# A graph block's head: the first linear layer in parts of 128, 256, 384 and 482 nodes, with its order of work written anew

## The chip, the cores and the metric

The kernel runs on one core of a Trainium2 chip, as a single launch. A core has a matrix engine (TensorE, PE in the profile; PEld is its loading of weights), a vector engine (VectorE, DVE), an activation engine (ScalarE, ACT), GpSimd (POOL) and SyncE (SP), which issues most of the DMAs here. Each runs its own queue of instructions and waits for the others by semaphores. The metric is the device time of the launch in microseconds (us).

## The reference

1250 nodes with 512 features go through a layer norm, a graph network of two layers with a linear layer ahead, a linear attention beside it, and a gated feed-forward layer. What the change touches is the beginning of this, the head:

```
xn  = _layernorm(x, axis=-1)                    # 1250 x 512
h   = xn @ lin_W.T + lin_b
h   = where(h > 0, h, lin_a * h)                # PReLU, the linear layer
for l in range(2):
    agg = segment_sum(h[src], dst, 1250)        # 41250 edges, sorted by dst
    h   = (h + agg) -> linear, PReLU, linear -> batch norm -> relu
k   = softmax over the nodes of (xn @ w_k) ...  # attention, uses xn too
```

The kernel turns the edge list into a dense matrix of 1250 x 1250 counts (adj, identity included), so that the sum over edges becomes a matrix product. For this it needs, of each block of 512 edges, its smallest and largest target node.

## The kernel before

**Tiles.** The nodes are cut in ten tiles of 128 (the last has 98). For a tile t, `x_first(t)` takes mean and variance (bn_stats and bn_aggr on VectorE, a Sqrt on ScalarE), `x_second(t)` makes scale and bias from them (a reciprocal and one more small step on VectorE) and normalizes the 128x512 tile on ScalarE into `xn`, and `x_third(t)` turns it: four transposes on TensorE into one PSUM bank and one ScalarE copy of 128x512 into `xn_t`, where features lie on the partitions (`to_features`, L602 to L607).

**Linear layer.** `lin(c0, cn, f)` (L710) computes output features f*128 to f*128+127 for the nodes from c0 to c0+cn: four products, which the chip runs as eight matmuls, into one bank, then `prelu` (L609): two ScalarE Relus from that bank (of the value and of its negative) and a VectorE step that joins them. It needs the copies in `xn_t` of all tiles from c0 to c0+cn. The nodes are taken in four parts, 256, 256, 384 and 354 wide, each for f from 0 to 3: sixteen calls.

**Edge chain.** Between them stand the steps that lead from the loaded edge list to the keys by which blocks are built: e_d, a cast of the targets on ScalarE (L746); smallest and largest target per partition on VectorE (L748 to L751); a transposition of both on TensorE (L759) and a reduction into `span` (L762); a transposition that spreads them over the partitions (L771, L772); from these base, base_i, low, key, s_hi and s_lo on VectorE and ScalarE (L766 to L794).

**Blocks.** `weave(us)` (L820) makes as many of the 81 edge blocks as are due: 0.70 blocks for each microsecond it is told. A block is two sets of one-hot rows, oh_s (4 of 128x128) and oh_k (4 of 128x240), made on VectorE; for every third block from the fifth on, oh_s comes from ScalarE instead (`source_rows`). Two made blocks are kept back (`keep=2`); then TensorE multiplies the oldest (four matmuls, L849) and VectorE adds it into adj (L851).

**Order.** From L718 (`given(engines={PE, DVE, Activation})`) to `head.close()` the order on TensorE, VectorE and ScalarE is the order in which the program is written: each of the three runs its own instructions of the head in that order, one behind the other. After `head.close()` the order is set by the framework. SP issues the loads at L653 to L675: tiles 0 and 1 of x, a quarter of the linear weights, tile 2, a quarter, tile 3, two quarters, the edges, tiles 4 to 9, and then weights of later stages. GpSimd clears adj (L685) and writes its diagonal. `stay_warm(n)` is n transposes of a constant on TensorE, read by nobody.

```
    for f in range(1, DT):
        weave(1.4)
        lin(512, 384, f)
        if f < 3:
            x_third(f + 7)
    head.close()
    for f in range(DT):
        weave(2.4)
        lin(896, 354, f)
```

Behind the head come the attention's products with wk, in whose midst most of the blocks are woven in (L878 and after).

Of the kernel before, what the change touches and what calls it, by code (L numbers as in the profile page):

```python
# [9 lines left out]
F32 = mybir.dt.float32  # L10
# [7 lines left out]
P = 128  # L18
N = 1250
D = 512  # L20
DT = D // P
# [20 lines left out]
CHUNKS = [(0, 418), (418, 416), (834, 416)]  # L42


def rows(t):
    return min(P, N - t * P)
# [479 lines left out]
def usual_block(  # L526
# [23 lines left out]
    nc = tc.nc  # L550
# [3 lines left out]
    tmp = ctx.enter_context(tc.tile_pool(name="tmp", bufs=2))  # L554
# [7 lines left out]
    def bank(dtype=F32):  # L562
        return psum.tile([P, 512], dtype, tag="bank", name="bank")

    def large(place, shape, dtype=F32, name="large"):

        return big.tile(shape, dtype, tag=place, name=name)

    def weight(src, name):
        w = wpool.tile([P, DT, D], F32, tag="w", name=name)  # L570
        nc.sync.dma_start(out=w, in_=src.rearrange("(c p) f -> p c f", p=P))
        return w

    def gemm(ps, cn, lhs, rhs, k=DT):
        for c in range(k):
            nc.tensor.matmul(ps[:, :cn], lhs(c), rhs(c), start=(c == 0), stop=(c == k - 1))  # L576
# [6 lines left out]
    def spread(src, n):  # L583

        st = small.tile([P, 6], F32, name="st")
        nc.vector.bn_stats(st[:n], src)  # L586
        mv = small.tile([P, 2], F32, name="mv")
        nc.vector.bn_aggr(mv[:n], st[:n])
        rs = small.tile([P, 2], F32, name="rs")
        nc.scalar.activation(rs[:n, 0:1], mv[:n, 1:2], AF.Sqrt, bias=eps[:n])  # L590
        return mv, rs

    def inverse(mv, rs, n):

        nc.vector.reciprocal(rs[:n, 0:1], rs[:n, 0:1])
        nc.vector.scalar_tensor_tensor(rs[:n, 1:2], mv[:n, 0:1], -1.0, rs[:n, 0:1],
                                       op0=ALU.mult, op1=ALU.mult)

    def normal(dst, src, rs, n):
        nc.scalar.activation(dst, src, AF.Identity, bias=rs[:n, 1:2], scale=rs[:n, 0:1])  # L600

    def to_features(dst, t, src, n):  # L602

        pt = bank()
        for c in range(DT):
            nc.tensor.transpose(pt[:, c * P:c * P + n], src[:, c * P:(c + 1) * P], ident[0:n, 0:n])  # L606
        nc.scalar.copy(dst[:, :, t * P:t * P + n], pt.rearrange("p (c n) -> p c n", c=DT)[:, :, 0:n])  # L607

    def prelu(dst, ps, cn, bias, slope):  # L609

        u = tmp.tile([P, CHUNKS[0][1]], F32, tag="xt", bufs=4, name="u")
        nc.scalar.activation(dst, ps[:, :cn], AF.Relu, bias=v(*bias))  # L612
        nc.scalar.activation(u[:, :cn], ps[:, :cn], AF.Relu, bias=minus(*bias), scale=-1.0)  # L613
        nc.vector.scalar_tensor_tensor(dst, u[:, :cn], minus(*slope), dst, op0=ALU.mult, op1=ALU.add)  # L614
# [13 lines left out]
    def v(name, i=0, n=1):  # L628
        at = _COLS[name][0] + i
        return v_sb[:, at:at + n]  # L630
# [4 lines left out]
    def minus(name, i=0):  # L635
        at = _COLS[name][0] + i
        return m_sb[:, at:at + 1]
# [48 lines left out]
    for t in range(NT):  # L686
        n = rows(t)
# [3 lines left out]
    xn = large("A", [P, NT, D], name="xn")  # L691
    xn_t = large("B", [P, DT, N], name="xn_t")
# [3 lines left out]
    def x_first(t):  # L696
        x_live[t] = spread(x_in[0:rows(t), t, :], rows(t))

    def x_second(t):
        n = rows(t)  # L700
        mv, rs = x_live.pop(t)
        inverse(mv, rs, n)
        normal(xn[0:n, t, :], x_in[0:n, t, :], rs, n)

    def x_third(t):
        to_features(xn_t, t, xn[0:rows(t), t, :], rows(t))

    h_t = large("C", [P, DT, N], name="h_t")

    def lin(c0, cn, f):  # L710
        ps = bank()
        gemm(ps, cn, lambda c: lw[:, c, f * P:(f + 1) * P], lambda c: xn_t[:, c, c0:c0 + cn])
        prelu(h_t[:, f, c0:c0 + cn], ps, cn, ("lin_b", f), ("lin_a", f))
# [3 lines left out]
    head = ExitStack()  # L717
# [3 lines left out]
    def stay_warm(n):  # L721
        for i in range(n):
            nc.tensor.transpose(idle[:, 0:P], ident, ident)

    stay_warm(22)
    x_first(0)
    x_first(1)
    x_second(0)
    x_second(1)
    x_third(0)  # L730
    x_third(1)
    stay_warm(3)
    x_first(2)
    x_second(2)
    x_first(3)
    x_second(3)
    lin(0, 256, 0)
    x_third(2)
    x_first(4)
    lin(0, 256, 1)  # L740
    x_third(3)
    x_second(4)
    x_first(5)
    lin(0, 256, 2)
    e_d = early.tile([P, NB, J], F32, name="e_d")
    nc.scalar.copy(e_d, edges[:, :, 1, :])  # L746
    ends = early.tile([P, 2, NB], F32, name="ends")
    nc.vector.tensor_reduce(ends[:, 0, :], e_d, AX.X, ALU.min)  # L748
    real = early.tile([P, NB, J], F32, name="real")
    nc.vector.scalar_tensor_tensor(real, e_d, float(N), e_d, op0=ALU.is_lt, op1=ALU.mult)  # L750
    nc.vector.tensor_reduce(ends[:, 1, :], real, AX.X, ALU.max)  # L751
    x_second(5)
    lin(0, 256, 3)
    x_third(4)
    x_first(6)
    pts = [bank(), bank()]
    lin(256, 256, 0)
    for k in range(2):
        nc.tensor.transpose(pts[k][0:NB, 0:P], ends[:, k, :], ident)  # L759
    span = early.tile([NB, 2], F32, name="span")  # L760
    for k, op in ((0, ALU.min), (1, ALU.max)):
        nc.vector.tensor_reduce(span[:, k:k + 1], pts[k][0:NB, 0:P], AX.X, op)  # L762
    x_second(6)

    s_hi = early.tile([P, NB, J], I32, name="s_hi")
    nc.vector.tensor_scalar(s_hi, edges[:, :, 0, :], 7, None, op0=ALU.logical_shift_right)  # L766
    lin(256, 256, 1)
    x_third(5)
    x_first(7)
    lows, highs = bank(), bank()  # L770
    nc.tensor.transpose(lows[:, 0:NB], span[:, 0:1].to_broadcast([NB, P]), ident[0:NB, 0:NB])  # L771
    nc.tensor.transpose(highs[:, 0:NB], span[:, 1:2].to_broadcast([NB, P]), ident[0:NB, 0:NB])  # L772
    base = const.tile([P, NB], F32, name="base")
    nc.vector.tensor_scalar(base, lows[:, 0:NB], float(N - W), None, op0=ALU.min)
    base_i = early.tile([1, NB], I32, name="base_i")
    nc.vector.tensor_copy(base_i, base[0:1, :])
    lin(256, 256, 2)
    x_third(6)
    x_second(7)
    low = const.tile([1, 2, NB], F32, name="low")  # L780
    nc.scalar.copy(low[:, 0, :], lows[0:1, 0:NB])
    nc.scalar.copy(low[:, 1, :], highs[0:1, 0:NB])
    key = e_d
    nc.vector.tensor_tensor(key, e_d, base.unsqueeze(2).to_broadcast([P, NB, J]), ALU.subtract)
    nc.vector.tensor_scalar(real, key, float(W), float(BIG), op0=ALU.is_ge, op1=ALU.mult)
    x_first(8)
    lin(256, 256, 3)
    nc.vector.tensor_tensor(key, key, real, ALU.add)
    nc.vector.scalar_tensor_tensor(key, s_hi, float(W), key, op0=ALU.mult, op1=ALU.add)
    x_second(8)  # L790
    x_first(9)
    lin(512, 384, 0)
    s_lo = early.tile([P, NB, J], F32, name="s_lo")
    nc.vector.scalar_tensor_tensor(s_lo, s_hi, -float(P), edges[:, :, 0, :], op0=ALU.mult, op1=ALU.add)  # L794
    x_third(7)
    x_second(9)

    def test_blocks():
# [14 lines left out]
    def source_rows(b, oh_s):  # L813

        off = hot.tile([P, J, P], F16, bufs=2, name="off")
        for j in range(J):
            nc.scalar.activation(off[:, j, :], count16[:, 0:P], AF.Abs, bias=s_lo[:, b, j:j + 1], scale=-1.0)
        nc.scalar.activation(oh_s, off, AF.Relu, bias=1.0, scale=-1.0)  # L818

    def weave(us, keep=2):  # L820

        state["due"] += us * PACE
        while state["block"] < min(NB, state["due"]):
            b = state["block"]
            state["block"] += 1
            oh_s = hot.tile([P, J, P], F16, name="oh_s")
            oh_k = hot.tile([P, J, NT * W], F16, name="oh_k")
            if b % 3 == 1 and b > 3:
                source_rows(b, oh_s)
            for j in range(J):  # L830
                if b % 3 != 1 or b <= 3:
                    nc.vector.tensor_scalar(oh_s[:, j, :], count16[:, 0:P], s_lo[:, b, j:j + 1], None,  # L832
                                            op0=ALU.is_equal)
                nc.vector.tensor_scalar(oh_k[:, j, :], count16, key[:, b, j:j + 1], None, op0=ALU.is_equal)  # L834
            held.append((b, oh_s, oh_k))
            drain(keep)
# [16 lines left out]

    PACE = 0.70

    for f in range(1, DT):
        weave(1.4)
        lin(512, 384, f)
        if f < 3:
            x_third(f + 7)  # L860
    head.close()
    for f in range(DT):
        weave(2.4)
        lin(896, 354, f)
    wo = weight(w_out, "wo")


# [186 lines left out]
    def q_third(t):  # L1054
        q, _ = q_live.pop(t)
        to_features(place["q_t"], t, q.rearrange("p h d -> p (h d)")[:rows(t)], rows(t))
# [207 lines left out]
    for t in range(NT):  # L1264
        n = rows(t)
# [95 lines left out]
    for t in range(NT):  # L1361
        n = rows(t)
# [60 lines left out]
def graph_block(tc, *args):  # L1423

    unusual = usual_block(tc, *args)
    with tc.If(unusual > 0):
        general_block(tc, *args)
# [58 lines left out]
```

## Time and profile before

Three runs: 574.11, 574.61 and 574.74 us, median 574.61. The profiled execution took 574.88 us, of which the span from first to last instruction is 572.9.

| | |
|---|---|
| mean granted TensorE clock | 0.981 |
| TensorE busy, 0 to 5, 5 to 10, 10 to 15 us | 3.40, 3.78, 5.00 |
| 15 to 20, 20 to 25, 25 to 30 us | 4.36, 2.56, 5.00 |
| 30 to 35, 35 to 40, 40 to 45 us | 5.00, 5.00, 4.91 |
| 45 to 50, 50 to 55, 55 to 60 us | 3.80, 5.00, 4.91 |
| first linear product | 8.71 us |
| first product with wk (behind the linear layer) | 57.71 us |
| VectorE busy, 60 to 70, 70 to 80, 80 to 90 us | 10.00, 9.76, 10.00 |

The first transposes of x start at 6.67 us, the first block is multiplied at 39.55, the blocks are done at 203. The window 25 to 30 is full on TensorE, but its granted clock there is 0.66; busy time alone doesn't tell that.

A profile's row gives start, duration and, in brackets, how long the engine had been idle before and what released it. ScalarE and VectorE overlap the end of one instruction with the start of the next by about a tenth of a microsecond, so what an instruction costs in a queue is the distance between two starts rather than its duration.

### The profile page before, as it was taken

The page shows a single profiled execution, that of the slowest core. Times are in us where ns is not written, and L with a number is a line of the kernel's source. Part 1 is how long each engine was busy: PE and PEld are TensorE (multiplying, and loading weights), DVE is VectorE, ACT ScalarE, POOL GpSimd, SP SyncE. Part 2 cuts the span into 40 slices and gives each one's busy share as a digit, 9 for nine tenths or more (in the row PEclk, how much of TensorE's full clock was granted, in tenths as well). Part 3 has the DMA queues.
Part 4 walks back from the last instruction along what each step waited for, and adds up shares of the span by engine and source line. Part 5 has one row for each costly group of instructions (what it writes and reads, how often), then busy time and mean ns, then how long its engine had stood idle before and what let it go on. Part 6 is the DMA issues. An engine that isn't in the chain of part 4 may idle for free.

```text
span 572.9 us, 6957 instructions
## 1 busy us (share of the span) xinstructions
PE 546.3 (95%) x2367; PEld 369.1 (64%) x2367; DVE 324.8 (57%) x1097; ACT 242.0 (42%) x533; POOL 80.1 (14%) x77
## 2 busy tenths in 40 slices
PE   8799999999999999999999999999999999997990
PEld 7665568799955477777854454459995557764540
DVE  4579999976899734444425534111113248708693
ACT  5676664454444112322333443113323456727242
POOL 7200000000000000000013331000000001106975
PEclk9899999999999999999999999999999999997995
DMA  9400200020030020000311002000009120402023
GB/s 287 176 1 1 74 2 1 1 74 2 1 113 36 0 74 0 1 1 1 111 37 52 22 1 73 0 0 1 2 0 348 55 74 1 146 1 75 0 76 110
DMA packets 19285, 29.10 MB, mean 51 GB/s; under 512 B 1529, under 2 KB 8185, under 8 KB 19240
## 3 DMA queue, kind: packets, MB, share of 16 engines
q1 hardware_dynamic: 18984, 28.32, 14.6%
q8 instruction: 20, 0.33, 0.2%
q10 hardware_dynamic: 256, 0.25, 0.2%
q14 instruction: 25, 0.20, 0.1%
HBM read 26.01 MB, written 2.56 MB: 50 GB/s over the span
## 4 chain that ended last, share of the span: by engine, by line
PE 87%; DVE 5%; ACT 3%; POOL 2%; issue 1%; DMA 1%; POOLq 0%; DVEq 0%; ACTq 0%
PE bank L576 28%; PE bank L981 16%; PE bank L968 12%; PE bank L917 6%; PE bank L1037 6%; PE bank L849 5%; PE bank L1064 5%; PE bank L1325 3%; PE bank L606 2%; PE bank L1374 1%; POOL m L1406 1%; POOL m L1407 1%; DVE st L586 1%; PE bank L902 1%; ACT xn L600 1%
## 5 line engine op out<-in xcount | busy, mean ns | idle before, releaser
L981 PE MATMUL bank<-adj,y_h 128*128 128x416 f32 (+1 forms) x240 | 86.5, 361 | 1.1 <-DVE adj L851 1.1
L981 PE MATMUL bank<-adj,y_l 128*128 128x416 f32 (+1 forms) x240 | 84.4, 352 | 0.0
L834 DVE TENSOR_SCALAR oh_k<-count,e_d 128x240 f16<-128x240 f16 x324 | 82.6, 274 | 0.0
L1083 POOL TENSOR_TENSOR m<-m,ls_bc 128x512 f32<-128x512 f32 (+1 forms) x10 | 12.7, 1269 | 447.3 <-ACT m L600 447.3
L968 PE MATMUL bank<-w,h_t 128*128 128x512 f32 (+1 forms) x160 | 70.4, 592 | 0.0
L576 PE MATMUL bank<-z_t,w 128*128 128x416 f32 (+1 forms) x192 | 68.9, 513 | 0.0
L576 PEld LDWEIGHTS bank<-z_t,w 128*128 128x128 f32 x192 | 36.1, 189 | 31.8 <-issue 29.9
L832 DVE TENSOR_SCALAR oh_s<-count,s_lo 128x128 f16<-128x128 f16 x220 | 54.1, 246 | 0.0
L968 PEld LDWEIGHTS bank<-w,h_t 128*128 128x128 f32 (+1 forms) x160 | 29.4, 188 | 34.8 <-issue 34.5
L614 DVE SCALAR_TENSOR_TENSOR z_t<-u,m_sb,z_t 128x416 f32<-128x416 f32 (+1 forms) x24 | 15.7, 653 | 59.8 <-ACT u L613 59.8
L981 PEld LDWEIGHTS bank<-adj,y_h 128*128 128x128 f32 x240 | 45.1, 188 | 2.6 <-issue 2.1
L981 PEld LDWEIGHTS bank<-adj,y_l 128*128 128x128 f32 x240 | 45.2, 188 | 1.2 <-issue 0.7
L849 PE MATMUL bank<-oh_k,oh_s 128*128 128x240 f16 x324 | 41.4, 266 | 1.4 <-ACT oh_s L818 1.2
L849 PEld LDWEIGHTS <-oh_s 128*128 128x128 f16 x324 | 31.6, 98 | 15.8 <-issue 5.1
L612 ACT ACTIVATE z_t<-bank,v_sb 128x416 f32<-128x416 f32 (+1 forms) x24 | 14.6, 608 | 61.5 <-PE bank L981 61.5
L851 DVE TENSOR_TENSOR adj<-adj,bank 128x240 f32 x81 | 32.3, 399 | 13.9 <-PE bank L849 12.5
L995 DVE BATCH_NORM_STATS2 bst<-bank 128x6 f32<-128x416 f32 (+1 forms) x24 | 14.4, 600 | 42.9 <-ACT h_t L994 42.9
L917 PE MATMUL bank<-kk,xn 128*128 128x128 f32 (+1 forms) x320 | 38.4, 275 | 0.0
L576 PE MATMUL bank<-xn_t,lw 128*128 128x256 f32 (+2 forms) x128 | 37.6, 439 | 0.3 <-ACT xn_t L607 0.3
L917 PEld LDWEIGHTS bank<-kk,xn 128*128 128x128 f32 (+1 forms) x320 | 37.0, 192 | 0.1
L1064 PE MATMUL bank<-mixer,q_t 128*128 128x512 f32 (+1 forms) x80 | 36.3, 592 | 0.0
L576 PE MATMUL bank<-xn_t,gw 128*128 128x256 f32 (+2 forms) x128 | 35.3, 427 | 0.9 <-ACT xn_t L607 0.9
(166 smaller groups left out, 800.0 us busy)
## 6 DMA issues: line engine op xcount, KB each, us to landing
t<-in_tv_w SPq DMA_DIRECT2D x12, 512.0 KB, 7.5
w<-in_conv_w SPq DMA_DIRECT2D x4, 1024.0 KB, 5.5
x_in<-in_x SPq DMA_DIRECT2D x9, 256.0 KB, 4.6
xt<-in_x SPq DMA_DIRECT2D x9, 256.0 KB, 4.1
out<-m SPq DMA_DIRECT2D x9, 256.0 KB, 2.4
rest<-in_tv_w SPq DMA_DIRECT2D x4, 512.0 KB, 4.8
lw<-in_lin_w SPq DMA_DIRECT2D x4, 256.0 KB, 4.9
wk<-in_w_qkv SPq DMA_DIRECT2D x1, 1024.0 KB, 7.0
```

The source lines that it names most:

```text
L576: nc.tensor.matmul(ps[:, :cn], lhs(c), rhs(c), start=(c == 0), stop=(c == k - 1))
L614: nc.vector.scalar_tensor_tensor(dst, u[:, :cn], minus(*slope), dst, op0=ALU.mult, op1=ALU.add)
L832: nc.vector.tensor_scalar(oh_s[:, j, :], count16[:, 0:P], s_lo[:, b, j:j + 1], None, op0=ALU.is_equal)
L834: nc.vector.tensor_scalar(oh_k[:, j, :], count16, key[:, b, j:j + 1], None, op0=ALU.is_equal)
L849: nc.tensor.matmul(ps[:, 0:NT * W], oh_s[:, j, :], oh_k[:, j, :], start=(j == 0), stop=(j == J - 1))
L851: nc.vector.tensor_tensor(adj_r[:, :, at], adj[:, :, at], ps[:, 0:NT * W].rearrange("p (s d) -> p s d", s=NT), ALU.add)
L917: nc.tensor.matmul(ps[:, c * P:(c + 1) * P], xn[0:n, t, c * P:(c + 1) * P], k_nodes(f)[0:n, t, :], start=(t == 0), stop=(t == NT - 1))
L968: nc.tensor.matmul(ps[:n], h_t[:, c, t * P:t * P + n], w1[:, c, :], start=(c == 0), stop=(c == DT - 1))
L981: nc.tensor.matmul(ps[:, :cn], y[0:n, s, f * P:(f + 1) * P], adj_r[0:n, s, c0:c0 + cn], start=(s == 0 and y is ys[0]), stop=(s == NT - 1 a ...
L1037: nc.tensor.matmul(ps[:n], xn_t[:, c, t * P:t * P + n], wq[:, c, :], start=(c == 0), stop=(c == DT - 1))
L1064: nc.tensor.matmul(ps[:n], q_t[:, h, t * P:t * P + n], mixer[:, h, :], start=(h == 0), stop=(h == DT - 1))
L1325: nc.tensor.matmul(ps[:, :cn], m1[:, c, f * P:(f + 1) * P], xn2_t[:, c, c0:c0 + cn], start=(c == 0), stop=(c == DT - 1))
```

## The change

The linear layer's parts are now 128, 256, 384 and 482 nodes wide. Tile 0 is brought to scale and normalized before tile 1's mean and variance are taken; its copy into `xn_t` is made by VectorE, and the first linear part follows it, before tiles 1 and 2 are turned. The other tiles' steps, the linear parts and the edge chain are given in a new order, in which the edge chain's steps stand earlier against the linear parts. Block 4's oh_s is made by VectorE (the condition is now b > 6). The weave has other amounts: 1.4, 1.4 and three times 3.0 where it was three times 1.4 and four times 2.4. The tile u in `prelu` is 512 wide, to hold the widest part; its slot in the pool was already as large. The hand-written order now reaches one call into the last part.

```diff
-    def to_features(dst, t, src, n):
+    def to_features(dst, t, src, n, copy=nc.scalar.copy):
...
-        nc.scalar.copy(dst[:, :, t * P:t * P + n], pt.rearrange("p (c n) -> p c n", c=DT)[:, :, 0:n])
+        copy(dst[:, :, t * P:t * P + n], pt.rearrange("p (c n) -> p c n", c=DT)[:, :, 0:n])
...
-        u = tmp.tile([P, CHUNKS[0][1]], F32, tag="xt", bufs=4, name="u")
+        u = tmp.tile([P, D], F32, tag="xt", bufs=4, name="u")
...
-    def x_third(t):
-        to_features(xn_t, t, xn[0:rows(t), t, :], rows(t))
+    def x_third(t, copy=nc.scalar.copy):
+        to_features(xn_t, t, xn[0:rows(t), t, :], rows(t), copy)
...
     stay_warm(22)
     x_first(0)
+    x_second(0)
     x_first(1)
-    x_second(0)
     x_second(1)
-    x_third(0)
+    x_third(0, nc.vector.tensor_copy)
+    stay_warm(2)
+    x_first(2)
+    lin(0, 128, 0)
+    x_second(2)
     x_third(1)
-    stay_warm(3)
-    x_first(2)
-    x_second(2)
+    lin(0, 128, 1)
     x_first(3)
+    lin(0, 128, 2)
+    x_third(2)
     x_second(3)
-    lin(0, 256, 0)
-    x_third(2)
-    x_first(4)
-    lin(0, 256, 1)
-    x_third(3)
-    x_second(4)
-    x_first(5)
-    lin(0, 256, 2)
+    lin(0, 128, 3)
     e_d = early.tile([P, NB, J], F32, name="e_d")
     nc.scalar.copy(e_d, edges[:, :, 1, :])
+    x_first(4)
+    lin(128, 256, 0)
+    x_third(3)
     ends = early.tile([P, 2, NB], F32, name="ends")
     nc.vector.tensor_reduce(ends[:, 0, :], e_d, AX.X, ALU.min)
...
     nc.vector.tensor_reduce(ends[:, 1, :], real, AX.X, ALU.max)
-    x_second(5)
-    lin(0, 256, 3)
-    x_third(4)
-    x_first(6)
+    x_second(4)
+    lin(128, 256, 1)
+    x_first(5)
     pts = [bank(), bank()]
-    lin(256, 256, 0)
     for k in range(2):
         nc.tensor.transpose(pts[k][0:NB, 0:P], ends[:, k, :], ident)
+    x_third(4)
     span = early.tile([NB, 2], F32, name="span")
     for k, op in ((0, ALU.min), (1, ALU.max)):
         nc.vector.tensor_reduce(span[:, k:k + 1], pts[k][0:NB, 0:P], AX.X, op)
-    x_second(6)
+    x_second(5)
+    lin(128, 256, 2)
+    x_first(6)
...
-    lin(256, 256, 1)
-    x_third(5)
-    x_first(7)
+    lin(128, 256, 3)
     lows, highs = bank(), bank()
...
+    x_third(5)
+    x_second(6)
     base = const.tile([P, NB], F32, name="base")
...
-    lin(256, 256, 2)
-    x_third(6)
-    x_second(7)
+    x_first(7)
+    lin(384, 384, 0)
     low = const.tile([1, 2, NB], F32, name="low")
...
+    x_third(6)
+    x_second(7)
     key = e_d
...
     x_first(8)
-    lin(256, 256, 3)
+    lin(384, 384, 1)
...
+    x_third(7)
     x_second(8)
     x_first(9)
-    lin(512, 384, 0)
+    lin(384, 384, 2)
...
-    x_third(7)
+    x_third(8)
     x_second(9)
...
-            if b % 3 == 1 and b > 3:
+            if b % 3 == 1 and b > 6:
                 source_rows(b, oh_s)
             for j in range(J):
-                if b % 3 != 1 or b <= 3:
+                if b % 3 != 1 or b <= 6:
...
+    weave(1.4)
+    lin(384, 384, 3)
+    x_third(9)
+    weave(1.4)
+    lin(768, 482, 0)
+    head.close()
     for f in range(1, DT):
-        weave(1.4)
-        lin(512, 384, f)
-        if f < 3:
-            x_third(f + 7)
-    head.close()
-    for f in range(DT):
-        weave(2.4)
-        lin(896, 354, f)
+        weave(3.0)
+        lin(768, 482, f)
     wo = weight(w_out, "wo")
```

## What it does to the time: the prediction

> **What bounds the kernel now.** I read the page's busy table first, then TensorE's waits before and after 60 us, then the order of time in the first 60 us, because all the changed lines run there. The page says that TensorE (PE) is nearly the whole span:
>
> ```profile
> PE 546.3 (95%) x2367; PEld 369.1 (64%) x2367; DVE 324.8 (57%) x1097; ACT 242.0 (42%) x533; POOL 80.1 (14%) x77
> ```
>
> So 26.6 of 572.9 us have no matmul. TensorE's waits from 0 to 60 us (total, count, longest):
>
> ```profile
> PE bank L771 <- DVE span L762: 2.4, 1, 2.4
> ...
> PE bank L849 <- ACT oh_s L818: 1.2, 1, 1.2
> PE bank L606 <- ACT xn L600: 0.8, 1, 0.8
> PE bank L759 <- DVE rs L595: 0.6, 1, 0.6
> ```
>
> From 60 to 220 us one wait is left, at the end of the blocks, so whatever the head loses on TensorE arrives at the end of the kernel one for one:
>
> ```profile
> PE bank L981 <- DVE adj L851: 1.1, 1, 1.1
> ```
>
> The largest wait is the edge chain's. In order of time on TensorE:
>
> ```profile
> 19.82 1.89 PE L576 MATMUL bank<-xn_t,lw 128*128 128x256 f32 x8
> 21.56 0.60 PE L606 MATMUL bank<-ident,xn 128*128 128x128 f32 x4
> 24.59 0.28 PE L771 MATMUL bank<-ident,span 81*128 81x81 f32 x1 [2.44 <-DVE span L762]
> ...
> 24.97 3.23 PE L576 MATMUL bank<-xn_t,lw 128*128 128x256 f32 x8
> 28.00 1.03 PE L606 MATMUL bank<-ident,xn 128*128 128x128 f32 x4
> ```
>
> After the pause the same eight matmuls take 3.23 us instead of 1.89. The busy table by windows has the reason (its first figure after the busy times is the granted clock):
>
> ```profile
> 22.00:25.40 3.40, 0.96 (x6) 1.00 0.00 0
> 25.40:28.85 3.45, 3.45 (x12) 0.51 0.00 0
> 28.85:33.00 4.15, 4.15 (x17) 1.00 0.01 4
> ```
>
> The pause costs twice: 2.6 us of nothing, then half a clock for 3.4 us, worth 1.7.
>
> **Unit costs**, from distances between starts. One linear part (eight matmuls) on TensorE: 256 wide 1.75 us, 384 wide 2.58, 354 wide 2.40, that is 0.84 ns a column and matmul; so 128 wide 0.88 and 482 wide 3.24. A tile's four transposes 0.44, one edge block 0.41. ScalarE (ACT), in order of time:
>
> ```profile
> 13.78 0.29 ACT L590 ACTIVATE rs<-mv,eps 128x1 f32<-128x1 f32 x1 [0.96 <-DVE mv L588]
> 13.98 0.46 ACT L612 ACTIVATE h_t<-bank,v_sb 128x256 f32<-128x256 f32 x1
> 14.34 0.46 ACT L613 ACTIVATE u<-bank,m_sb 128x256 f32<-128x256 f32 x1
> 14.69 0.58 ACT L607 COPY xn_t<-bank 128x512 f32<-128x512 f32 x1
> 15.62 0.82 ACT L600 ACTIVATE xn<-x_in,rs 128x512 f32<-128x512 f32 x1 [0.35 <-DVE rs L596]
> ```
>
> The next starts 0.20 after a Sqrt, 0.36 after a 256-wide Relu (0.46 after a 384-wide), 0.72 after a normalization, 0.46 after a copy. For VectorE (DVE): bn_stats 0.72, reciprocal to the bias 0.19, PReLU's last step 0.40 at 256. These queues run the head strictly in program order: VectorE's reciprocal of tile 4 starts at 15.24, behind PReLU's step of 14.84, though its input was there at 14.07.
>
> A 128-wide Relu has no row. The line through 0.46 (256) and 0.57 (384) gives 0.35, 0.25 to the next. The Trainium skill speaks against small parts here ("ScalarE: Activation LUTs", section What ACT_TABLE_LOAD costs): 335 cycles of fixed cost beside one per column at 1.2 GHz, overlapping by 93 ns. An estimate by it is 0.39 at 128 wide, 0.29 to the next. But it makes 0.49 of the 256-wide one that measures 0.46, so I take the row; the rule would add 0.04 to each of eight Relus, 0.3 us. The one copy of tile 0 on VectorE has as nearest row a 128x512 VectorE operation reading PSUM (0.69, L1042); its bounds are the ScalarE copy's 0.58 and 0.76 (the 512-wide L1312).
>
> **The head after, walked by hand.** TensorE's work hardly changes: four groups of 1.75+1.75+2.58+2.40 become 0.88+1.75+2.58+3.24, 0.1 us less in all; one warm-up transpose less (0.1). What changes is what it waits for. Starts and ends in us:
>
> - Tile 0 no longer waits behind tile 1's bn_stats: reciprocal 5.08, normalization 5.47 to 6.28, transposes at 6.33 (before 6.67: gain 0.33). VectorE takes the copy only behind tile 1's scale and bias, 7.02 to 7.71. First linear part at 7.77 (before 8.71), second 9.09 after tile 1's transposes.
> - Now the queues bite. Tile 2's normalization is queued behind the first part's two Relus (8.80 to 9.41) and PReLU's VectorE step (9.45): it runs 10.12 to 10.93. Tile 1's copy is behind it (10.84 to 11.42), the second part's Relus behind that, bn_stats of tile 3 behind their VectorE step (12.22), its Sqrt (13.16) behind that, the third part's Relus next, and then tile 2's copy, 13.86 to 14.44. TensorE has finished the four narrow parts at 12.30 (4 x 0.88 is all the work tile 0 gives) and needs tiles 1 and 2: it starts the 128..384 part at 14.50. **Wait 2.2.**
> - e_d is cast at 15.89 (before 17.42). Its two reductions follow the first 128..384 part's PReLU on VectorE and end at 20.1; TensorE has been through since 18.44. **Wait 1.7**, then 0.9 for tile 4's normalization, which is queued behind the same reductions (20.42 to 21.23).
> - The second chain step costs nothing now: the span is ready at 24.08, TensorE comes at 25.22. The 2.6 us pause is gone, as meant.
> - But tile 5's transposes (25.5 to 25.94) are followed on TensorE directly by the 384-wide part, which needs their copy. That copy stands behind tile 6's Sqrt (27.31) and the fourth part's Relus (27.51 to 28.33): it ends at 28.81. **Wait 2.9.**
> - Then parts at 28.87, 31.89 and 34.91 with one tile's transposes between; tile 8's normalization (38.2 to 39.0) comes late, **wait 1.6**; the fourth part 39.5 to 42.08; tile 9, and its copy behind the Relus at 43.22, **wait 1.3**; the 482-wide part at 43.76.
>
> From there before and after have the same kind of work. Before, the last linear part starts its group at 43.68 with three blocks multiplied, and all four are done at 56.67 with eight. After: 4 x 3.24 + 7 x 0.41 = 15.8, done at 59.6 with seven. The wait of 1.2 for block 4's rows goes, since VectorE now makes them, for 4 x 0.16 = 0.64 us more of VectorE. Difference 59.6 - 56.67 + 0.41 for the missing block = **+3.3 us**.
>
> **The clock.** Here row and rule part. The row: a pause of 2.6 us ending at 24.6 was followed by half clock for 3.4 us. The pause before the 384-wide part is 2.9. The Trainium skill ("TensorE: Matmul & The Clock Gate", section What's actually happening) has the clock fall after an idle window of about 3.4 us; by its words neither pause is a whole window, and the sum stays +3.3. By the row the first 384-wide part runs 3.4 us at half clock: 28.87 to 33.15 instead of 31.45, **+1.7**, and as its Relus feed the chain all behind it shifts. I take the row, as it is this kernel's: **+5.0**. Falls after the pauses at 14.5 and 20.2 may come too; they are hidden, for ScalarE comes to those results 0.1 to 2 us later than TensorE has them even at half clock. The bounds are 0 and +3.4 (a second fall in the open).
>
> **Other steps.** No DMA is moved in the head; on SP only wo's load, which waits for the linear weights' buffer, starts later by the same amount, and its reader comes at 127 us, some 70 us of cover. The last edge piece is issued at 6.1 and lands 5.5 later, before the cast at 15.9. POOL moves nothing; it is done at 17.9, before any block is added. The pace after the head makes 1.4 blocks less before it (11.8 x 0.7 against 13.8 x 0.7), so block 80 falls to the last of the 512-wide steps, where VectorE idles 2.7 us near 198: 0, at worst +1. VectorE is full from 60 to 100 us in the page's second part; it starts blocks 4 to 5.6 us later, but has 1.4 blocks (2.4 us) less to make by the k stage, so it trails TensorE: 0, at worst +1.5.
>
> Sum against the profiled execution, 574.88 in all (span 572.9): 579.9. The median of the runs shown is 0.27 lower: **579.6**.
>
> **Rivals.**
> 1. *Walk right, no clock fall* (or one that is partly hidden): +3.3, 577.9. For it: the fall depends on where the pause lies.
> 2. *VectorE becomes the bound of the block phase*: +5.0 and 1.5 more, 581.1. For it, the full digits; against it, TensorE's eight matmuls and eight block products follow each other every 3.63 us without a gap.
> 3. *Faster*: the copies get through. If ScalarE's queue is nearly free, TensorE pays at the three places only the bare path from transposes to copy to the next part, 0.16 + 0.04 + 0.58 + 0.06 = 0.85 each, and 0.77 at the start: 6.33 + 41.9 of work + 3.3 = 51.6, plus 0.41, against 56.67: -4.7, 569.9. It decides from where the new waits total less than 8.0 us; I count 11.4 without the clock. Against it: every link of the chain is program order that the trace before already obeys.
> 4. *Even*: waits of 7 to 9 us, 574.6.
>
> **Numbers.** Main case 0.42, rival 1 0.23, rival 2 0.10, rival 3 0.18, even 0.07. What this kernel's runs can tell from no change is about 0.2%, 1.15 us. Faster 0.18, same 0.06, slower 0.76. The main case's own range is 577 to 582; the range for 8 in 10 reaches down into the faster side, 572.5 to 581.8.
>
> **What would show it.** Right: TensorE waits for ScalarE's xn_t copy (L607) before the first 256-wide and the first 384-wide part, 2 to 3 us each; clock near 0.5 around 29 to 32; no long wait at L771; the first wk product near 61 to 63 (57.7 before). Wrong: these copies wait under 1 us, or the 482-wide part starts before 42.

## The result, and the profile after

The changed kernel takes 582.3 us (580.83 to 584.13, four runs), the kernel before, on the same chip, 574.39: a ratio of 1.0139 with a 95% interval from 1.0118 to 1.016, that is 7.9 us more. The direction was forecast, the size was not: +5.0 was written down, and 582.3 lies half a microsecond above the range of 572.5 to 581.8.

The profiled execution took 581.43 us with a span of 579.1, 6.2 more than before. Nearly the whole of it is there when the linear layer ends: the first product with wk starts at 63.51 instead of 57.71, and 36 matmuls of blocks are done by then instead of 39, which is three quarters of a block: 5.8 + 0.3 = 6.1. Behind it next to nothing is won or lost: a long product near the end (L1328, L1325 before) starts at 527.95 instead of 521.91, 6.0 later. The busy table of the page after:

```profile
PE 546.6 (94%) x2366; PEld 366.6 (63%) x2366; DVE 326.3 (56%) x1102; ACT 241.3 (42%) x527; POOL 80.2 (14%) x77
```

TensorE has the same 546 us of work, in a longer span. Its waits from 0 to 75 us (total, count, longest):

```profile
PE bank L576 <- ACT xn_t L607: 6.3, 3, 2.8
PE bank L606 <- ACT xn L600: 3.3, 4, 1.5
...
PE bank L757 <- DVE ends L748: 0.8, 1, 0.8
...
PE bank L757 <- DVE ends L751: 0.5, 1, 0.5
```

The long wait for the span is gone. In its place stand 9.6 us of waits for ScalarE, for its copies (L607) and for its normalizations (L600), where the kernel before had 1.1. In order of time on TensorE (start, duration, what it is, idle time before it and what ended that):

```profile
7.74 1.16 PE L576 MATMUL bank<-xn_t,lw 128*128 128x128 f32 x8 [0.57 <-DVE xn_t L607]
...
14.65 1.99 PE L576 MATMUL bank<-xn_t,lw 128*128 128x256 f32 x8 [1.98 <-ACT xn_t L607]
...
27.11 0.23 PE L770 MATMUL bank<-ident,span 81*128 81x81 f32 x1
...
29.35 2.85 PE L576 MATMUL bank<-xn_t,lw 128*128 128x384 f32 x8 [1.50 <-ACT xn_t L607]
...
39.90 0.66 PE L606 MATMUL bank<-ident,xn 128*128 128x128 f32 x4 [1.54 <-ACT xn L600]
...
46.75 3.50 PE L576 MATMUL bank<-xn_t,lw 128*128 128x482 f32 x8 [2.80 <-ACT xn_t L607]
...
63.51 2.98 PE L576 MATMUL bank<-xn_t,wk 128*128 128x418 f32 x8
```

The start of the linear layer is a microsecond earlier than before, and that is lost at the very next width: the first 256-wide part waits for tile 2's copy. The transposition of the span at 27.11 has no wait. Each later width begins with a wait for ScalarE, and the largest stands where the forecast had a small one, before the 482-wide part. What ScalarE did in these microseconds, in order of time:

```profile
42.23 0.40 ACT L820 ACTIVATE off<-count,s_lo 128x128 f16<-128x128 f16 x1 [0.62 <-DVE s_lo L797]
42.54 0.80 ACT L600 ACTIVATE xn<-x_in,rs 98x512 f32<-98x512 f32 x1
43.25 2.15 ACT L820 ACTIVATE off<-count,s_lo 128x128 f16<-128x128 f16 x7
45.30 0.57 ACT L612 ACTIVATE h_t<-bank,v_sb 128x384 f32<-128x384 f32 x1
45.76 0.57 ACT L613 ACTIVATE u<-bank,m_sb 128x384 f32<-128x384 f32 x1
46.23 0.47 ACT L607 COPY xn_t<-bank 128x392 f32<-128x392 f32 x1
```

Rows of off (`source_rows`, L820 in this kernel) run on both sides of tile 9's normalization, seven of them between it and the copy of its transposition. They belong to blocks 7 and 10, which the program makes behind `head.close()`. The seven hold up the two Relus and the copy by 2 us, and TensorE waits for that copy.

The clock of the same execution, in windows (start and end in us; the window's length, TensorE's busy time, its instructions, the granted clock; then the DMA share and GB/s):

```profile
18.00:21.40 3.40, 1.46 (x6) 1.00 1.04 386
21.40:24.90 3.50, 3.33 (x10) 0.51 0.14 48
28.90:32.30 3.40, 2.95 (x11) 1.00 0.01 2
```

A fall is a stretch in which the granted clock goes to about half. There is one of some 3.4 us in the head, as before, but under the last two 256-wide parts, where TensorE would have waited for ScalarE anyway, and not under the first 384-wide part.

### The profile page after: what moved, and what is told of

Same layout as the page of the kernel before. It is cut to its first block, busy times and chain, and to the rows that moved or that the text cites. A ratio compares the mean times of both kernels' runs of the same rounds, so it can differ in the third digit from the quotient of the medians.

```text
span 579.1 us, 6954 instructions
## 1 busy us (share of the span) xinstructions
PE 546.6 (94%) x2366; PEld 366.6 (63%) x2366; DVE 326.3 (56%) x1102; ACT 241.3 (42%) x527; POOL 80.2 (14%) x77
## 4 chain that ended last, share of the span: by engine, by line
PE 86%; DVE 5%; ACT 4%; POOL 2%; issue 1%; DMA 1%; POOLq 0%; DVEq 0%; ACTq 0%
PE bank L576 27%; PE bank L984 16%; PE bank L971 12%; PE bank L920 6%; PE bank L1040 6%; PE bank L852 6%; PE bank L1067 5%; PE bank L1328 3%; PE bank L606 2%; PE bank L1377 1%; POOL m L1409 1%; POOL m L1410 1%; DVE st L586 1%; ACT xn L600 1%; ACT u L613 1%
## 5 line engine op out<-in xcount | busy, mean ns | idle before, releaser
L835 DVE TENSOR_SCALAR oh_s<-count,s_lo 128x128 f16<-128x128 f16 x224 | 56.2, 251 | 0.0
L576 PE MATMUL bank<-xn_t,lw 128*128 128x128 f32 (+3 forms) x128 | 37.7, 441 | 6.8 <-ACT xn_t L607 6.3
L852 PE MATMUL bank<-oh_k,oh_s 128*128 128x240 f16 x324 | 40.2, 266 | 0.0
```

Of the source, the lines that this page charges most:

```text
L852: nc.tensor.matmul(ps[:, 0:NT * W], oh_s[:, j, :], oh_k[:, j, :], start=(j == 0), stop=(j == J - 1))
```

## The experiments

Two theories went in. The first, that the head is set by the chain of queued ScalarE and VectorE steps, with the block rows at 42 us as the term that was missed. The second, that the excess is the clock: more or longer falls than the one that was counted. A third question was which of the old kernel's own pauses were worth anything.

### The changed kernel once more

No edit: the kernel of the change, with a blank line at its end.

> The changed kernel once more, as the base of this set. If its spread of 580.8 to 584.1 us comes from the place at which TensorE's clock falls (sometimes under a part that everything waits for), its times fall again into two groups about 2 to 2.5 us apart, and the lower group shows a mean clock of 0.981, the upper 0.977. If the spread is anything else, times and clock are not tied to each other.

Measured: 581.64 us (581.23 to 582.52, four runs), ratio 1.0125 (1.0111 to 1.014). The spread is 1.3, so two groups more than 2 apart are not seen. Over both sets of this kernel, though, time and clock go together: the four runs with a mean clock of 0.981 or more took 580.83 to 581.43 us, the four with 0.977 to 0.980 took 582.03 to 584.13. And the profiled execution of this set, one of the second kind, has its clock falls at other places. On TensorE in order of time:

```profile
29.47 2.85 PE L576 MATMUL bank<-xn_t,lw 128*128 128x384 f32 x8 [2.54 <-ACT xn_t L607]
...
46.85 6.28 PE L576 MATMUL bank<-xn_t,lw 128*128 128x482 f32 x8 [2.79 <-ACT xn_t L607]
...
530.80 18.52 PE L1328 MATMUL bank<-xn_t,m 128*128 128x418 f32 x48 [2.63 <-DVE m L1315]
```

and in windows:

```profile
15.00:18.80 3.80, 3.80 (x13) 0.56 1.04 378
...
21.40:24.90 3.50, 2.73 (x16) 1.00 0.04 13
...
45.20:48.60 3.40, 1.75 (x2) 0.57 0.00 0
48.60:52.00 3.40, 3.40 (x6) 0.50 0.00 0
```

The first fall comes at 15 instead of 21.4, and yet the 384-wide part starts within 0.12 us of the other execution: 29.47 against 29.35. Where ScalarE's copy is late, a slow TensorE only shortens its own wait (1.50 with the fall just ahead of it, 2.54 without). A second fall begins at 45.6, still in the 2.8 us pause, and ends at 52.5. The first 482-wide part lies under it, in the open: 6.28 instead of 3.50. The 2.8 us lost there are still lost at 530.80. In the other execution the same row reads

```profile
527.95 19.78 PE L1328 MATMUL bank<-xn_t,m 128*128 128x418 f32 x48 [2.62 <-DVE m L1315]
```

Here a late fall, which both have, is half as long in the second (3.6 against 7.0 us), and the product takes 18.52 instead of 19.78. So the two spans differ by 1.5 only.

### The block rows kept out of the head

The rows read a copy of s_lo which ScalarE makes behind tile 9's copy, so that they can't run ahead of it. The buffer `real` is free by then.

```diff
-            nc.scalar.activation(off[:, j, :], count16[:, 0:P], AF.Abs, bias=s_lo[:, b, j:j + 1], scale=-1.0)
+            nc.scalar.activation(off[:, j, :], count16[:, 0:P], AF.Abs, bias=real[:, b, j:j + 1], scale=-1.0)
...
     x_third(9)
+    nc.scalar.copy(real, s_lo)
     weave(1.4)
     lin(768, 482, 0)
```

> Only the eight ScalarE rows of blocks 7 and 10 (L820, 2.3 us in all) are kept behind tile 9's copy; they read s_lo through a copy made there. Theory (these rows, written behind the head but running in it, hold the last Relus and tile 9's copy): the first 482-wide part starts at 44.7 instead of 46.75 and the span is 2.0 us shorter than that of the changed kernel. Rival (the rows only fill time in which ScalarE waits anyway, tile 9 itself is late): less than 0.4 us.

Measured: 578.18 us (577.43 to 579.65, six runs), ratio 1.0071 (1.0057 to 1.0085), 3.5 less than the changed kernel beside it. ScalarE in order of time:

```profile
42.59 0.81 ACT L600 ACTIVATE xn<-x_in,rs 98x512 f32<-98x512 f32 x1 [0.88 <-DVE rs L596]
43.31 0.56 ACT L612 ACTIVATE h_t<-bank,v_sb 128x384 f32<-128x384 f32 x1
43.77 0.57 ACT L613 ACTIVATE u<-bank,m_sb 128x384 f32<-128x384 f32 x1
44.23 0.48 ACT L607 COPY xn_t<-bank 128x392 f32<-128x392 f32 x1
44.60 0.48 ACT L862 COPY real<-s_lo 128x324 f32<-128x324 f32 x1
45.10 2.44 ACT L820 ACTIVATE off<-count,real 128x128 f16<-128x128 f16 x8
```

and TensorE:

```profile
44.77 3.50 PE L576 MATMUL bank<-xn_t,lw 128*128 128x482 f32 x8 [0.76 <-ACT xn_t L607]
```

The Relus now stand directly behind the normalization, the copy is 2.0 us earlier, and so is the 482-wide part (44.77 against 46.75). That is 2.0 of the 3.5. The rest fits the second fall: the pause in which it began is 0.76 instead of 2.8, this execution has a clock of 1.00 from 44 to 60 us, and none of the six runs has a mean clock under 0.981, as four of the changed kernel's eight have. What is left over before, 578.18 - 574.48 = +3.7, is near the +3.3 of the walk.

### The waits filled with transposes

The same kernel as changed, with constant transposes that nobody reads in TensorE's longest waits (14, 6, 4, 6, 11, 12 and 22 of them), to keep it from standing still.

```diff
+    def fill(n):
+        spare = bank()
+        for i in range(n):
+            nc.tensor.transpose(spare[:, 0:P], ident, ident)
...
     lin(0, 128, 3)
+    fill(14)
...
     x_first(7)
+    fill(11)
     lin(384, 384, 0)
...
     weave(1.4)
+    fill(22)
     lin(768, 482, 0)
```

> TensorE's waits in the head are filled with transposes that nobody reads, each filling shorter than the wait it stands in. Theory (TensorE's clock falls after these waits, in a window whose place differs from run to run): no fall in the head after 10 us, the runs lie within 1 us of each other, at or below the lower group of the changed kernel (about 0.5 us below, as the 256-wide parts at 22 to 25 us run at full clock). Rival (the spread is not the clock's): spread of 2 us or more stays. If the fillings cost more than they save, the time rises.

Measured: 580.17 us (579.05 to 580.84, five runs), ratio 1.0098 (1.0085 to 1.0111). Its profile shows a clock of 1.00 through the whole head:

```profile
10.00:60.00 50.00, 47.02 (x250) 1.00 0.24 83
```

So far as this one execution stands for the five runs, the falls in the head are worth about 1.5 us of the median (581.64 - 580.17), and 5.7 us over the kernel before stay. The spread did not shrink as expected (1.8). The clock is a part of the loss, not its bulk.

### The old kernel with block 4's rows on VectorE

```diff
-            if b % 3 == 1 and b > 3:
+            if b % 3 == 1 and b > 6:
                 source_rows(b, oh_s)
             for j in range(J):
-                if b % 3 != 1 or b <= 3:
+                if b % 3 != 1 or b <= 6:
```

> The kernel before with one edit of the change alone: block 4's source rows on VectorE. Theory of the prediction: TensorE's wait of 1.2 us for these rows goes, the time falls by up to 1.2 us. Rival: VectorE, which is full from there on, takes 0.64 us more and TensorE waits for the next blocks instead: between 0 and +0.6.

Measured: 574.0 us (573.15 to 574.78, 14 runs), ratio 0.999 (0.9983 to 0.9998): -0.5, less than half of the 1.2 that could have gone. The wait of 1.2 for ScalarE's rows is replaced by 0.4 for oh_k. This profile answers another question in passing. It has the 2.4 us pause of the kernel before, on TensorE in order of time:

```profile
24.44 0.28 PE L771 MATMUL bank<-ident,span 81*128 81x81 f32 x1 [2.45 <-DVE span L762]
...
24.82 1.93 PE L576 MATMUL bank<-xn_t,lw 128*128 128x256 f32 x8
...
29.34 2.85 PE L576 MATMUL bank<-xn_t,lw 128*128 128x384 f32 x8 [0.42 <-ACT xn_t L607]
```

but no fall behind it (1.93, not 3.23). And at full speed TensorE runs into a wait for ScalarE's copy, 0.42, soon after: where the fall had been, ScalarE was close behind.

### The old kernel without its pause

The transpositions of the span, with base behind them, go behind one more linear part.

```diff
     x_third(5)
-    x_first(7)
+    lin(256, 256, 2)
     lows, highs = bank(), bank()
...
-    lin(256, 256, 2)
     x_third(6)
+    x_first(7)
     x_second(7)
```

> The kernel before with only the pause taken out: the two transpositions L771 and L772 stand behind the third 256-wide part of the second group, tile 7's mean and variance behind tile 6's turn. If the pause is worth what the prediction said, 2.6 us and 1.7 of half clock, the time falls by 4.3. If ScalarE's chain of Relus and copies follows closely behind it, about 2.3. If that chain is the bound there, nothing.

Measured: 574.44 us (573.9 to 575.34, 13 runs) against 574.65, ratio 1.0001 (0.9993 to 1.0009): nothing. TensorE's waits from 0 to 75 us:

```profile
PE bank L606 <- ACT xn L600: 1.4, 3, 0.8
PE bank L849 <- ACT oh_s L818: 1.2, 1, 1.2
PE bank L771 <- DVE span L762: 0.8, 1, 0.8
```

The pause is 0.8 instead of 2.4, but the waits for normalizations have gone from 0.8 to 1.4, a clock fall still comes at 26 to 29.8, and the last linear group begins at 43.94 (before 43.68). The pause in the old kernel was slack in a head that ScalarE and VectorE set.

### Tile 0 alone, in the old kernel

```diff
     x_first(0)
-    x_first(1)
     x_second(0)
+    x_first(1)
     x_second(1)
-    x_third(0)
+    x_third(0, nc.vector.tensor_copy)
     x_third(1)
```

> The kernel before with tile 0 normalized alone and copied by VectorE, parts of 256 as before. Theory: the first transposes start 0.3 us earlier, but tile 1 waits behind the copy, and a 256-wide part needs both: first linear product at 9.1 instead of 8.7, time 0 to +0.5. Rival (an early start pays by itself): -0.3.

Measured: 575.11 us (573.99 to 575.91, 21 runs), ratio 1.0007 (1.0001 to 1.0014): +0.5, as expected. A 256-wide first part needs tile 1 too, which is now later: it starts at 9.30 instead of 8.71.

### The first wait taken out

The kernel with the late rows (not shown again), and in it the copies of tiles 1 and 2 given ahead of the narrow parts' Relus that stood before them.

```diff
     x_first(2)
-    lin(0, 128, 0)
-    x_second(2)
     x_third(1)
-    lin(0, 128, 1)
+    x_second(2)
     x_first(3)
-    lin(0, 128, 2)
+    lin(0, 128, 0)
+    lin(0, 128, 1)
     x_third(2)
     x_second(3)
+    lin(0, 128, 2)
     lin(0, 128, 3)
```

> The late rows of the last set, and one more move: tile 1's copy, tile 2's normalization and copy are given before the Relus of the narrow parts that stood ahead of them. Theory (the changed head is bound by the order in ScalarE's and VectorE's queues): the first 256-wide part starts at 12.4 instead of 14.65 us, the later links of the chain shift with it, and the time falls by 2.2 us against the late rows alone (578.2), to 576. Rival (the queues' order matters at this place only, the next wait takes it back): below 0.8 us.

Measured: 575.85 us (575.2 to 576.69, eight runs), ratio 1.0028 (1.0018 to 1.0038), 2.3 less than the kernel it was made from. On TensorE:

```profile
27.14 2.85 PE L576 MATMUL bank<-xn_t,lw 128*128 128x384 f32 x8 [1.50 <-ACT xn_t L607]
...
42.46 3.50 PE L576 MATMUL bank<-xn_t,lw 128*128 128x482 f32 x8 [0.76 <-ACT xn_t L607]
```

The 384-wide part is 2.3 earlier (29.45 there), the 482-wide part 2.3 (44.77), the end 2.3. One wait removed in the queue's order moves all that follows by its whole length: this is a chain, and the parts' widths are the same.

### All steps one tile ahead

The changed kernel's parts, late rows and VectorE copy; each tile's mean, scale and normalization stands one step earlier against the linear parts, and the first copies stand as in the run above. The cut shows added lines only.

```diff
+    x_first(4)
+    lin(0, 128, 2)
     lin(0, 128, 3)
+    x_second(4)
+    x_first(5)
     e_d = early.tile([P, NB, J], F32, name="e_d")
...
+    lin(128, 256, 0)
+    x_third(3)
+    x_second(5)
     lin(128, 256, 1)
+    x_third(4)
+    lin(128, 256, 2)
     pts = [bank(), bank()]
...
     lin(384, 384, 0)
+    x_third(6)
+    x_second(8)
+    x_first(9)
```

> The parts of the change (128, 256, 384, 482, tile 0 alone, VectorE's copy, block 4) with every normalization and copy given one tile ahead of the Relus, and the late rows. Theory (not the parts but the order in the queues costs the time): the first 384-wide part starts near 22 us (29.4 in the changed kernel, where half its work is done), the first 482-wide part near 35 (46.75), and the time is below the kernel before, near 570.5. Rival (narrow first parts starve TensorE whatever the order, as 128 nodes give it 3.5 us of work for two tiles' preparation): the first 384-wide part after 26 us, the time at or above 574.5.

Measured: 571.31 us (569.55 to 573.36, six runs), ratio 0.9947 (0.9928 to 0.9965): 3.3 less than the kernel before. On TensorE:

```profile
22.64 2.79 PE L576 MATMUL bank<-xn_t,lw 128*128 128x384 f32 x8
...
36.73 5.20 PE L576 MATMUL bank<-xn_t,lw 128*128 128x482 f32 x8 [1.91 <-ACT xn_t L607]
```

The 384-wide part starts 6.7 us earlier than in the changed kernel, and without a wait for its copy. Of the long waits one is left, 1.91 before the 482-wide part, with a clock fall over that part in this execution (5.20); the waits for normalizations are down to 1.2 in all.

### The last copy ahead of the Relus

As the kernel above, with tile 9's transposes and copy between the fourth 384-wide part and its Relus. `lin` is split for that.

```diff
-    lin(384, 384, 3)
+    ps_3 = lin_sum(384, 384, 3)
     x_third(9)
+    lin_out(ps_3, 384, 384, 3)
     nc.scalar.copy(real, s_lo)
```

> The version with everything one tile ahead, and tile 9's copy given before the Relus of the fourth 384-wide part, which it does not need. Theory (the last wait there, 1.9 us before the first 482-wide part, is again a copy behind Relus in ScalarE's queue, and it can bring a fall of the clock over that part): the wait falls to 1 us, the time from 571.3 to 570.4 or, with fewer falls in the open, 570. Rival (the wait is off the path or another wait follows): no change.

Measured: 570.8 us (569.74 to 571.19, six runs), ratio 0.9933 (0.9919 to 0.9947), the lowest median of all. On TensorE:

```profile
36.20 3.50 PE L576 MATMUL bank<-xn_t,lw 128*128 128x482 f32 x8 [0.97 <-ACT xn_t L607]
```

The wait is halved and no fall follows it in this profile. The gain over the version above, 0.5, is inside the two spreads. The narrower spread fits a fall that has gone (two of the six runs above have a mean clock of 0.981, the slowest two, and here none is under 0.983), but that was not shown run by run.

### The same manner with the old widths

Parts of 256, 256, 384 and 354, late rows, the steps given ahead as far as I could work it out for these widths. The cut is against the kernel before.

```diff
     lin(0, 256, 0)
     x_third(2)
-    x_first(4)
+    x_second(3)
     lin(0, 256, 1)
+    x_first(4)
     x_third(3)
+    lin(0, 256, 2)
+    lin(0, 256, 3)
     x_second(4)
     x_first(5)
```

> The same order with everything one tile ahead, but with the parts of the kernel before (256, 256, 384, 354), so that the first part needs two tiles. If the narrow first part is worth its earlier start (7.8 against 8.7 to 9.1 us), the time is 0.9 to 1.5 us above 571.3. If the parts' widths do not matter beside the order of the queues, within 0.5 us of it. If narrow parts are a burden in themselves (they give TensorE too little work for the preparation of the next tiles), below 571.

Measured: 576.68 us (574.43 to 578.89, 18 runs), ratio 1.0032 (1.0021 to 1.0043): slower than the kernel before, and 5.4 above the same manner with the narrow first part. None of the three expected cases has this. TensorE's waits from 0 to 75 us show where:

```profile
PE bank L606 <- ACT xn L600: 4.5, 5, 1.9
PE bank L576 <- ACT xn_t L607: 1.9, 3, 1.2
```

and in order of time on ScalarE and TensorE:

```profile
19.68 0.81 ACT L600 ACTIVATE xn<-x_in,rs 128x512 f32<-128x512 f32 x1 [0.82 <-DVE rs L596]
...
30.68 6.33 PE L576 MATMUL bank<-xn_t,lw 128*128 128x384 f32 x16 [0.41 <-ACT xn_t L607]
```

ScalarE's normalization of tile 4 comes only at 19.68, because its VectorE steps stand behind the fourth part's PReLU, and tile 6 has to be turned and copied before the 384-wide part, which starts at 30.68. This order was my own and had not been tuned as the old one is, so the run doesn't show that wide parts are slower. What a well-tuned order would make of the old widths stays open. That the narrow start is no burden in itself is shown by the runs with all steps ahead, which have it and are faster than the kernel before.

## Why the prediction was off in size

**The bound and the mechanism: right.** The walk along the queues gave the starts 14.50, 28.87 and 39.5 for the first 256-wide part, the first 384-wide part and the fourth; measured were 14.65, 29.35 and 40.39. The waits it named before the first two are there, 1.98 for 2.2 and 1.50 for 2.9 (2.54 where no fall stood just ahead). The run with the first wait taken out and the one with all steps ahead show that these waits come from the order in ScalarE's and VectorE's queues, and not from the widths.

**"These queues run the head strictly in program order": the step that failed.** The head's own instructions do. But the framework placed eight rows of two later blocks, written behind the head, into ScalarE's stream as soon as s_lo was there, ahead of tile 9's copy. The walk had 43.76 for the 482-wide part; it started at 46.75, and 2.0 of these 3.0 us go when the rows are held back. The trace before shows such rows, there of blocks 4 and 7, between the Relus and copies of its own head:

```profile
37.41 0.40 ACT L817 ACTIVATE off<-count,s_lo 128x128 f16<-128x128 f16 x1 [0.61 <-DVE s_lo L794]
...
39.81 0.70 ACT L817 ACTIVATE off<-count,s_lo 128x128 f16<-128x128 f16 x2
...
41.70 1.58 ACT L817 ACTIVATE off<-count,s_lo 128x128 f16<-128x128 f16 x5
```

There they held up nothing that TensorE was waiting for: tile 9's copy ended at 41.83, and TensorE came to it at 43.68. I had read the order of the code there and not that of the trace.

**The wait "1.3 before the 482-wide part" became 2.8,** and in the second profile of the changed kernel a clock fall that began in it nearly doubled that part (6.28 instead of 3.50). Holding the rows back saved 3.5 in the median, 1.5 more than the shift; that this is the missing fall fits the two profiles and the mean clocks of the runs, but was not shown run by run.

**The clock, +1.7: the place was wrong, and that the size is near is luck.** The fall was put under the first 384-wide part. In both profiles of the changed kernel that part runs at full clock, and what was named as a sign of being right, a clock near 0.5 around 29 to 32, is not there (1.00). The falls stand elsewhere, and taking those of the head away saves 1.5. The rule of the Trainium skill weighed against the row ("TensorE: Matmul & The Clock Gate", section What's actually happening: a fall needs a whole idle window of about 3.4 us) made the term zero. The trace does not agree with it: in the 3.4 us ahead of the fall at 21.4 TensorE was busy for 1.46. Rival 1, the walk without a fall at 577.9, is out too: with no fall in the head of its profile the kernel with filled waits still took 580.17.

**"The pause costs twice": wrong as a price.** 2.6 and 1.7 us were what the old trace showed on TensorE, but moving that pause away gained nothing (1.0001). This error did not enter the sum, since the new waits were walked, but it may have made the faster side look more open than it was.

**Block 4's rows:** the 1.2 us wait went, as said; in the old kernel alone the edit brings 0.5, and 0.4 comes back as a wait for VectorE's rows.

**Small terms held.** The 128-wide Relus took 0.35 to 0.37 us, 0.25 to 0.27 apart, as the line through the rows said; VectorE's copy 0.69; the first part started at 7.74 (7.77). Rival 2 is out: from 75 to 225 us TensorE has only the old wait at the end of the blocks, 1.1 us.

Against the profiled execution: +3.3 of the walk, 2.0 of rows, and some 1.0 of drift up to 42 us, about 0.4 of it the clock (in the run with filled waits the fourth 384-wide part starts at 40.02 instead of 40.39), make 6.3; the span grew by 6.2. The other 0.6 of the drift is spread over the chain and has no cause shown. The medians differ by more, 7.9 in the first set of runs and 7.2 in the second. Further falls in the open would explain that: the second profile has one, and the slower half of the runs has the lower mean clock.

## What to carry to other kernels

An engine at 42% of the span can set the bound of a stage: where queues are in order, walk every instruction of the slow engines, and see for each copy that the bottleneck needs what stands ahead of it. Take that order from the trace, with the instructions that a framework brings in from later code, and not from the program alone. Before a pause is priced, ask who is next behind it: a wait in the profile is only worth as much as the next latest engine leaves of it.

## What the runs showed of the hardware that was not expected

The clock falls after a pause, but not each time, not at one place, and not always for the same time. After a pause of 2.44 us the kernel before fell to 0.51 for some 3.4 us; the old kernel with block 4's rows on VectorE, after 2.45 us, did not fall. The changed kernel fell at 21.4 in one execution, at 15.0 and at 45.6 in another, the last time for 6.9 us, although TensorE worked without a pause through the second half of it. None of these falls needed 3.4 us without work: in the 3.4 us ahead of them TensorE was busy for 0.96 us in the kernel before and for 1.46 to 1.60 in the changed one.

The mean granted clock of a whole run says how much half clock there was, but not where. Every profile here has a late fall between 515 and 535 us too, of some 7 us in all but one, and another behind TensorE's last matmul, which costs TensorE nothing. One fall of 3.4 us moves the mean of 573 us by 3.4 x 0.5 / 573 = 0.003. Still, more half clock goes with more time: with block 4's rows on VectorE, runs at 0.989 took 573.15 and 573.17 us, those at 0.981 573.96 to 574.78. In the changed kernel it depends on where the fall comes: runs of 581.23 and 581.26 had 0.981 and 0.986, since a fall there is often hidden behind a wait for ScalarE, and only the runs at 0.980 and below are longer.
